# A quantized weight made strip by strip: other steps for the side work of a strip, and later stores in the last one

## The chip, the cores and the metric

The kernel runs on one core of a Trainium2 chip. Its metric is the device time of one execution in microseconds. The core has five engines that run their own instruction lists in order: TensorE (PE in the profile, with its weight loads as PEld), VectorE (DVE), ScalarE (ACT), GpSimd (POOL) and SyncE (SP), which here only issues DMAs. Engines wait for each other by semaphores.

## The reference, cut to what matters

```python
# cond: x (4096 tokens x 2048), weight (2048 x 2048), codebook of 32 values
delta = lora_B @ lora_A * (32 / 64)
wg = (weight + delta).reshape(O, I // 128, 128)
normalized = wg / exp(scale_log)                   # a scale for each group of 128
idx = searchsorted(thresholds, normalized)         # thresholds: middles of the sorted codebook
quantized = codebook[idx]
w = (quantized - normalized) + normalized          # the straight-through form
w_eff = (w * scale).reshape(O, I) + delta
y = x @ w_eff.T
# ffn
result = y @ W_base.T + bias
probs = softmax(y @ router.T)                      # 8 experts
mixed = sum over experts of probs * (y @ A.T @ core)
out = x + result + (mixed @ B.T) * 2
```

All of it is computed in 32 bits. As nothing non-linear lies between y and W_base, the kernel multiplies the two weights first, and the tokens with the product afterwards.

## The kernel before, in words

**First stage.** The 2048 x 2048 quantized weight is made in 16 strips of 128 columns (NS = 16, loop `for i in range(NS)`, line 755). A strip is one tile `w` of 128 partitions x 16 groups x 128, that is 128 x 2048 numbers, with a second tile `a` for the result. Tiles `a` are three, tiles `w` two.

The codebook lookup is a series of 31 selects: for each threshold r, ScalarE writes a mask of 8 bits ("above", line 549: a scaled Relu that is positive where w is over the threshold), and VectorE overwrites `a` with the next codebook value where the mask is set (`copy_predicated`, line 550). There are four mask buffers. Of strip i VectorE does r = 4 to 30, 27 selects of 128 x 2048, in `quantize` (line 554). The levels r = 0 to 3 are done while the strip before is quantized, in halves of 8 groups (f = 0 and 1), by ScalarE and GpSimd: `scalar_level` (lines 512 to 524: Relu, Sign, and a scaled copy, on ScalarE), `pool_levels` (lines 534 and 535) and `last_level` (539). In strips 6 to 15 the level r = 3 of the second half is left to VectorE as a select of half size at the strip's beginning (`half_step`).

**What a strip needs first.** `load_w` (line 391) fetches w by SP's queue; `delta` (404) multiplies the low-rank factors of one half on TensorE into the tile `d`, of which there is one in PSUM, so that the second half has to wait until ScalarE has read the first; `scaled` (498) is that read, into `a`; `normalize` (504) adds it to w and multiplies by the inverse scale on GpSimd (lines 506 and 429).

**What a strip needs after.** `straight_through` (564) does subtract, add and multiply (lines 572 to 574) on GpSimd in two halves, in the last strip on VectorE in four quarters. Then `products` (742) multiplies the strip on TensorE with the four 512-column blocks b of W_base, in pairs (2, 0) and (3, 1), each in four chunks c of four groups (`multiply`, line 614, matmuls at line 621). The first chunk of a pair needs the groups 0 to 3 of `a`. Blocks 0 and 1 of W_base stay in SBUF; 2 and 3 are streamed again for each strip, one piece a chunk, in three buffers (`load_piece`, line 487). A pair ends with `low_rank` (606), the low-rank part of the product, at line 609. `keep` (652) copies a finished block out of PSUM on ScalarE and stores it to DRAM. `multiply_router`, `router_parts`, `router_sum` and `keep_router` do the same for the router's few columns, `route` (671) multiplies them with tokens. There are three PSUM banks for the tiles of the pairs and the router.

**Order by hand.** `at` is a table of steps; `behind(r, f, ...)` puts a call at step r, and `quantize` makes the calls of step r just after it has issued the mask and select of level r + 4. While strip i is quantized, its steps hold: the preparation of strip i + 1, the products of strip i - 1, the end of the products of strip i - 2 (its last chunk stands before step 0), and, from strip 5 on, one column block of finished strips that is taken through sums on GpSimd (`outer_w`, `inner_pair`) and stored by SP (`put`, three DMAs or five a pair). Each engine gets its instructions in this order, and waits in it.

**After the last strip** (lines 843 to 870) come its products, evacuations and stores, `late_columns` for blocks 0 and 2 of the last four strips, and the second stage begins: tokens times the combined weight, 196 products in a twofold scheme of seven (a fast matrix multiplication), bound to TensorE. The sums for blocks 1 and 3 (lines 1190 to 1204) are still done then.

Of the kernel before, what the change touches and what calls it, by code (L numbers as in the profile page):

```python
# [21 lines left out]
P = 128  # L22
# [6 lines left out]
NL = 4  # L29
# [154 lines left out]
def adaln_ffn_kernel(  # L184
# [29 lines left out]
    nc = tc.nc  # L214
    D, N = xT.shape
    NS, _, NM, _ = weight.shape
# [34 lines left out]
    strip = [j * NK + k for k in range(NK) for j in range(4)]  # L251
# [114 lines left out]
    with ExitStack() as sa:  # L366
# [195 lines left out]
            assert not at, at  # L562

        def straight_through(i):
            last = i == NS - 1
            n = 4 if last else 2
            for h in range(n):
                m = ts(h, NM // n)
                w, a = strips[i]["w"][:, m, :], strips[i]["a"][:, m, :]
                sc = scale[:, strip[i], m].unsqueeze(2).to_broadcast([P, NM // n, P])  # L570
                v = nc.vector if last else nc.gpsimd
                v.tensor_tensor(a, a, w, ALU.subtract)  # L572
                v.tensor_tensor(a, a, w, ALU.add)  # L573
                v.tensor_tensor(a, a, sc, ALU.mult)  # L574
# [70 lines left out]
        def router_parts(i):  # L645
            nc.scalar.copy(raw, strips[i]["r"][:, 0:P])

        def router_sum(i):

            nc.tensor.matmul(strips[i]["r"][:, P : P + RP], raw, stack, start=True, stop=True)  # L650

        def keep(i, b):
            out = spool.tile([P, 4, BC], F32, tag="out", name=f"out_{i}_{b}")
            nc.scalar.copy(out.rearrange("p q c -> p (q c)"), strips[i][b])  # L654
            (nc.scalar if i == NS - 1 else nc.sync).dma_start(wc_dram[i // 4][b][:, i % 4], out)

        def keep_router(i):
            nc.scalar.copy(rac[:, strip[i], :], strips[i]["r"][:, P : P + RP])
# [83 lines left out]
        def products(i, bs, c):  # L742

            for b in bs:
                multiply(i, b, c)
            if c == NC - 1:
                low_rank(i, bs)
# [7 lines left out]
        for i in range(NS):  # L755
            at = {}

            def behind(r, f, *args):
                at.setdefault(r, []).append(lambda: f(*args))

            if i > 1:

                products(i - 2, (3, 1), NC - 1)
                route(i - 2, 0)
                behind(0, load_route, i - 2, 1)
                behind(2, keep, i - 2, 3)
                behind(3, keep, i - 2, 1)
            if i + 1 < NS:
                delta(i + 1, 0)
                if i > 0:  # L770
                    behind(1, load_w, i + 1, 2)
                behind(4, scaled, i + 1, 0)
                behind(4, normalize, i + 1, 0)
                behind(10, scaled, i + 1, 1)
                behind(10, normalize, i + 1, 1)
                for r, f, parts in ((0, 0, (11, 12, 13)), (NL - 1, 0, (14, 15, 18)), (0, 1, (19, 20, 21))):
                    for n, p in enumerate(parts):
                        behind(p, scalar_level, i + 1, f, r, n)
                behind(14, pool_levels, i + 1, 0)
                behind(19, last_level, i + 1, 0)  # L780
                behind(21, pool_levels, i + 1, 1)
            if i > 0:


                behind(9, load_route, i - 1, 0)
                if i == NS - 1:
                    behind(9, load_route, i - 1, 1)
                for c in range(2):
                    behind(2 + 3 * c, products, i - 1, (2, 0), c)
                if i + 1 < NS:  # L790
                    behind(7, delta, i + 1, 1)
                if i > 1:
                    behind(8, route, i - 2, 1)
                for c in range(2, NC):
                    behind(2 + 3 * c, products, i - 1, (2, 0), c)
                behind(13, multiply_router, i - 1)
                behind(16, keep, i - 1, 2)
                behind(17, keep, i - 1, 0)
                for c in range(NC - 1):
                    behind((17, 20, 22)[c], products, i - 1, (3, 1), c)  # L800
                behind(19, router_sum, i - 1)
                behind(23, keep_router, i - 1)
                behind(18, router_parts, i - 1)
                if i + 2 < NS:
                    behind(20, load_la, i + 2)
            else:
                behind(3, nc.vector.reciprocal, rflat[:, NM:], flat[:, NM:])
                behind(7, delta, i + 1, 1)
                behind(22, lora_columns, 0)
                behind(24, lora_columns, 1)  # L810
                behind(25, lora_router)
            for n, (g, b) in enumerate(made.get(i, [])):
                step_of = (3, 5, 10, 13, 17, 23, 25) if len(made[i]) == 1 else (
                    (4, 6, 8, 9, 10, 12, 13) if n == 0 else (17, 19, 21, 22, 23, 24, 25)
                )

                def begin(g, b):
                    columns(
                        g, b,
                        ypool.tile([P, 2048], F32, tag="up", name=f"up_{g}_{b}"),  # L820
                        ypool.tile([P, 1536], F32, tag="more", name=f"more_{g}_{b}"),
                    )
                    fetch(g, b)

                def inner_pair(g, b, ms):
                    z = zp.tile([P, 1024], F32, tag="z", name=f"z_{g}_{b}_{ms[0]}")
                    inner_some(nc.gpsimd, g, b, ms, z)

                behind((0, 14)[n], begin, g, b)
                r = step_of  # L830
                behind(r[0], outer_w, nc.gpsimd, g, b)
                behind(r[1], inner_pair, g, b, PAIRS[0])
                behind(r[1], inner_pair, g, b, PAIRS[1])
                behind(r[2], put, g, b, PAIRS[0])
                behind(r[3], put, g, b, PAIRS[1])
                behind(r[4], inner_pair, g, b, PAIRS[2])
                behind(r[4], inner_pair, g, b, PAIRS[3])
                behind(r[5], put, g, b, PAIRS[2])
                behind(r[6], put, g, b, PAIRS[3])
            quantize(i, at)  # L840
            straight_through(i)

# [12 lines left out]
        for bs in ((2, 0), (3, 1)):  # L855
            for c in range(NC):
                products(last, bs, c)
            if bs[0] == 2:
                multiply_router(last)
                router_parts(last)  # L860
            for b in bs:
                keep(last, b)
            if bs[0] == 2:
                router_sum(last)
                keep_router(last)
                late_columns()
        for h in range(2):
            route(last, h)
        for h in range(2):
# [411 lines left out]
```

## Time and profile before

| | us |
|---|---|
| median of three runs | 2672.97 (2670.01 to 2674.29) |
| the profiled execution | 2666.77 |
| its span | 2665.0 |

| engine | busy us (share) |
|---|---|
| TensorE | 2503.9 (94%) |
| VectorE | 1549.0 (58%) |
| GpSimd | 1367.2 (51%) |
| ScalarE | 1130.1 (42%) |

The page's second part cuts the span in 40 slices of 66.6 us with the busy share of each in tenths. Its fifth part has a row for each group of equal instructions: line, engine, operation, output and input, how many; behind the bar the busy time, the mean of one in ns, and the idle time before them with what ended most of it. A view of waits sums them by who waited for whom: total us, how often, the longest. The chain of waits follows the work that ended last back through its releasers: start, us, what. A timeline has start, us, engine, line, operation and how many were merged; in brackets, the idle time before and what ended it.

### The profile page before, as it was taken

What the parts mean: (1) busy time and instruction counts of PE and PEld (TensorE: products, weight loads), DVE (VectorE), ACT (ScalarE), POOL (GpSimd) and SP (SyncE); (2) the same over time, 40 slices, a digit from 0 to 9 for tenths busy, and PEclk for the clock granted to TensorE, in tenths of its full rate; (3) what the DMA queues carried; (4) which work ended last, traced back from release to release, by engine and by line L of the source; (5) the groups of instructions that cost most, each with busy time, mean ns of one, the idle gap of its engine ahead of it and who ended that gap; (6) DMA issues with size and microseconds to landing.
All of it is one profiled execution on the core that took longest, in us unless ns stands there. A gap on an engine that the chain in (4) does not pass through costs nothing.

```text
span 2665.0 us, 26423 instructions
## 1 busy us (share of the span) xinstructions
PE 2503.9 (94%) x10576; PEld 1704.1 (64%) x10576; DVE 1549.0 (58%) x990; ACT 1130.1 (42%) x796; POOL 1367.2 (51%) x783
## 2 busy tenths in 40 slices
PE   5499999999999999999999999999999999999999
PEld 2244444444444444345888888888888888888887
DVE  9999999999999999973433223242133332224221
ACT  7899999999999999930000000000000000000000
POOL 5777778889888888745313140042320323202224
PEclk9799999999999999999999999999999999999999
DMA  8255457776777777699844666536675455854554
GB/s 317 102 177 185 168 181 252 233 241 228 234 243 249 235 231 227 217 327 347 323 174 173 218 245 232 187 142 213 244 234 194 157 206 177 279 208 173 194 199 158
DMA packets 225979, 581.08 MB, mean 218 GB/s; under 512 B 20600, under 2 KB 121728, under 8 KB 182720
## 3 DMA queue, kind: packets, MB, share of 16 engines
q1 hardware_dynamic: 219296, 557.96, 61.1%
q0 software_dynamic: 4960, 14.95, 1.6%
q10 hardware_dynamic: 1600, 6.49, 0.7%
q8 instruction: 83, 1.36, 0.2%
q14 instruction: 40, 0.33, 0.0%
HBM read 477.62 MB, written 101.71 MB: 217 GB/s over the span
## 4 chain that ended last, share of the span: by engine, by line
PE 62%; ACT 17%; DVE 8%; POOL 7%; DMA 3%; issue 2%; SPq 0%; DVEq 0%; ACTq 0%; POOLq 0%
PE z L954 49%; ACT above L549 11%; PE m L621 10%; DVE a L550 7%; ACT sg L516 2%; ACT sg L519 2%; POOL a L572 1%; POOL a L573 1%; PE z L984 1%; ACT a L521 1%; POOL lv L534 1%; POOL a L574 1%; POOL a L535 1%; DMA xA<-in_xT 1%; DMA wc_dram<-out 1%
## 5 line engine op out<-in xcount | busy, mean ns | idle before, releaser
L550 DVE COPY_PREDICATED a<-above,step 128x2048 f32<-128x2048 uint8 (+1 forms) x448 | 1090.2, 2436 | 61.1 <-ACT above L549 19.3
L549 ACT ACTIVATE above<-w,neg_t 128x2048 fp8e5<-128x2048 f32 (+1 forms) x448 | 872.4, 1976 | 55.1 <-DVE a L550 44.5
L954 PE MATMUL z<-t,s 128*128 128x256 f32 x3584 | 791.4, 380 | 2.0 <-DVE u L1036 1.7
L954 PEld LDWEIGHTS z<-t,s 128*128 128x128 f32 x3584 | 677.5, 190 | 105.5 <-issue 13.2
L621 PE MATMUL m<-wbp,a 128*128 128x512 f32 x1024 | 502.1, 636 | 115.0 <-POOL a L574 101.0
L621 PE MATMUL m<-wb,a 128*128 128x512 f32 x1024 | 462.1, 594 | 4.4 <-ACT out L654 4.4
L621 PEld LDWEIGHTS m<-wbp,a 128*128 128x128 f32 x1024 | 202.6, 204 | 370.9 <-issue 239.7
L621 PEld LDWEIGHTS m<-wb,a 128*128 128x128 f32 x1024 | 194.5, 191 | 247.1 <-issue 242.4
L1034 ACT COPY m<-z 128x1024 f32<-128x1024 f32 x28 | 28.4, 1013 | 759.2 <-PE z L954 759.2
L1045 POOL TENSOR_TENSOR c<-u,m 128x1024 f32<-128x1024 f32 x16 | 50.1, 3130 | 443.8 <-DVE u L1042 422.4
L954 PE MATMUL z<-xA,s 128*128 128x256 f32 x1152 | 254.6, 379 | 0.0
L534 POOL TENSOR_SCALAR lv<-w,past,rise 128x1024 f32<-128x1024 f32 x65 | 245.9, 3783 | 3.7
L954 PEld LDWEIGHTS z<-xA,s 128*128 128x128 f32 x1152 | 218.8, 190 | 30.5 <-issue 0.8
L1045 POOL TENSOR_TENSOR M<-u,m 128x1024 f32<-128x1024 f32 x8 | 24.5, 3068 | 328.9 <-DVE u L1042 288.2
L954 PE MATMUL z<-xC,s 128*128 128x256 f32 x768 | 169.7, 379 | 0.0
L954 PE MATMUL z<-xB,s 128*128 128x256 f32 x768 | 169.7, 379 | 0.0
L535 POOL TENSOR_TENSOR a<-a,lv 128x1024 f32<-128x1024 f32 x65 | 154.3, 2374 | 27.1 <-ACT a L521 21.0
L1036 DVE TENSOR_TENSOR u<-z,m 128x1024 f32<-128x1024 f32 x28 | 34.3, 1224 | 218.5 <-issue 175.0
L1040 ACT COPY m<-z 128x1024 f32<-128x1024 f32 x28 | 28.3, 1011 | 308.8 <-PE z L954 308.8
L954 PEld LDWEIGHTS z<-xC,s 128*128 128x128 f32 x768 | 145.9, 190 | 19.8
L954 PEld LDWEIGHTS z<-xB,s 128*128 128x128 f32 x768 | 145.9, 190 | 19.8
L1042 DVE TENSOR_TENSOR u<-z,u 128x1024 f32<-128x1024 f32 x28 | 34.3, 1223 | 119.8 <-PE z L954 81.3
(213 smaller groups left out, 1958.0 us busy)
## 6 DMA issues: line engine op xcount, KB each, us to landing
s<-s_dram SPq DMA_DIRECT2D x196, 1024.0 KB, 4.9
wbp<-in_wbT SPq DMA_DIRECT2D x131, 1024.0 KB, 5.4
xs<-in_xT SPq DMA_DIRECT2D x64, 512.0 KB, 6.5
xA<-in_xT SPq DMA_DIRECT2D x24, 1024.0 KB, 9.4
s_dram<-z SPq DMA_DIRECT2D x84, 256.0 KB, 6.2
xB<-in_xT SPq DMA_DIRECT2D x16, 1024.0 KB, 10.4
outT<-M SPq DMA_DIRECT2D x16, 1024.0 KB, 12.5
w<-in_weight SPq DMA_DIRECT2D x30, 512.0 KB, 5.2
```

Of the source, the lines that this page charges most:

```text
L516: nc.scalar.activation(strips[i]["sg"], q, AF.Relu, bias=neg_t[:, r : r + 1], scale=GAIN)
L519: nc.scalar.activation(sg, sg, AF.Sign)
L534: v.tensor_scalar(lv, half(i, f, "w"), past[:, r : r + 1], rise[:, r : r + 1], ALU.is_gt, ALU.mult)
L535: v.tensor_tensor(a, a, lv, ALU.add)
L549: nc.scalar.activation(above[:, c], q, AF.Relu, bias=neg_t[:, r : r + 1], scale=GAIN, saturate=False)
L550: nc.vector.copy_predicated(a, above[:, c].bitcast(U8), step[:, r : r + 1].to_broadcast([P, F // n]))
L621: nc.tensor.matmul(ps, strips[i]["a"][:, CM * c + m, :], t[:, m, :], start=c == 0 and m == 0, stop=False)
L954: nc.tensor.matmul(z[:, c, :], s[:, k, ts(c, P)], rhs[:, k, :], start=not more and k == 0 and c % PER == 0, stop=k == NK - 1 and c % PER = ...
L1034: nc.scalar.copy(temp("m1", o), z["a"])
L1036: nc.vector.tensor_tensor(temp("u2", o), z["b"], state["m1", o], ALU.add)
L1042: nc.vector.tensor_tensor(temp("u3", o), z["d"], state["u2", o], ALU.add)
L1045: lambda d: nc.gpsimd.tensor_tensor(d, state["u3", o], state["m5", o], ALU.add),
```

## The change

Four things change, all in the first stage.

1. `straight_through`: GpSimd does the first half in two parts of four groups, the second half whole.
2. Steps. The second half's `delta` goes from step 7 to step 3, `scaled` to 3 and 5 (before 4 and 10), both halves of `normalize` to 6 (before 4 and 10). The level r = 0 of the first half goes to 9, 10, 11, that of the second half to 13, 16, 17, the level 3 of the first half to 20, 21, 23, and GpSimd's levels to 11 and 17, with `last_level` at 23. The chunks of the pair (2, 0) go to 4, 6, 8, 11 (before 2, 5, 8, 11), and that pair's evacuations to 14 and 15 (before 16 and 17).
3. A column's `outer_w` goes from step 3 to 5, its pairs to 8, 14 and twice 24 (before 5, 5, 17, 17), its puts to 10, 16, 25, 26 (before 10, 13, 23, 25). In strip 15, which has two columns, the steps keep their values.
4. `keep` is split into `evacuate` and `store`. In the last strip both blocks of a pair are evacuated first. The stores of the first pair, the router's sum and `late_columns` come behind the first chunk of the second pair.

```diff
         def straight_through(i):
             last = i == NS - 1
-            n = 4 if last else 2
-            for h in range(n):
-                m = ts(h, NM // n)
+            v = nc.vector if last else nc.gpsimd
+            for m in (0, 4), (4, 8), *(((8, 12), (12, 16)) if last else ((8, 16),)):
+                n = m[1] - m[0]
+                m = slice(*m)
                 w, a = strips[i]["w"][:, m, :], strips[i]["a"][:, m, :]
-                sc = scale[:, strip[i], m].unsqueeze(2).to_broadcast([P, NM // n, P])
-                v = nc.vector if last else nc.gpsimd
+                sc = scale[:, strip[i], m].unsqueeze(2).to_broadcast([P, n, P])
...
-        def keep(i, b):
+        def evacuate(i, b):
             out = spool.tile([P, 4, BC], F32, tag="out", name=f"out_{i}_{b}")
             nc.scalar.copy(out.rearrange("p q c -> p (q c)"), strips[i][b])
-            (nc.scalar if i == NS - 1 else nc.sync).dma_start(wc_dram[i // 4][b][:, i % 4], out)
+            strips[i]["out", b] = out
+
+        def store(i, b, q=nc.sync):
+            q.dma_start(wc_dram[i // 4][b][:, i % 4], strips[i]["out", b])
+
+        def keep(i, b):
+            evacuate(i, b)
+            store(i, b)
...
                 behind(2, keep, i - 2, 3)
-                behind(3, keep, i - 2, 1)
+                behind(4, keep, i - 2, 1)
             if i + 1 < NS:
                 delta(i + 1, 0)
                 if i > 0:
                     behind(1, load_w, i + 1, 2)
-                behind(4, scaled, i + 1, 0)
-                behind(4, normalize, i + 1, 0)
-                behind(10, scaled, i + 1, 1)
-                behind(10, normalize, i + 1, 1)
-                for r, f, parts in ((0, 0, (11, 12, 13)), (NL - 1, 0, (14, 15, 18)), (0, 1, (19, 20, 21))):
+                behind(3, scaled, i + 1, 0)
+                behind(3, delta, i + 1, 1)
+                behind(5, scaled, i + 1, 1)
+                for f in range(2):
+                    behind(6, normalize, i + 1, f)
+                for r, f, parts in ((0, 0, (9, 10, 11)), (0, 1, (13, 16, 17)), (NL - 1, 0, (20, 21, 23))):
                     for n, p in enumerate(parts):
                         behind(p, scalar_level, i + 1, f, r, n)
-                behind(14, pool_levels, i + 1, 0)
-                behind(19, last_level, i + 1, 0)
-                behind(21, pool_levels, i + 1, 1)
+                behind(11, pool_levels, i + 1, 0)
+                behind(17, pool_levels, i + 1, 1)
+                behind(23, last_level, i + 1, 0)
...
                 for c in range(2):
-                    behind(2 + 3 * c, products, i - 1, (2, 0), c)
-                if i + 1 < NS:
-                    behind(7, delta, i + 1, 1)
+                    behind((4, 6, 8, 11)[c], products, i - 1, (2, 0), c)
...
-                behind(16, keep, i - 1, 2)
-                behind(17, keep, i - 1, 0)
+                behind(14, keep, i - 1, 2)
+                behind(15, keep, i - 1, 0)
                 for c in range(NC - 1):
                     behind((17, 20, 22)[c], products, i - 1, (3, 1), c)
-                behind(19, router_sum, i - 1)
-                behind(23, keep_router, i - 1)
+                behind(20, router_sum, i - 1)
+                behind(24, keep_router, i - 1)
...
-                step_of = (3, 5, 10, 13, 17, 23, 25) if len(made[i]) == 1 else (
-                    (4, 6, 8, 9, 10, 12, 13) if n == 0 else (17, 19, 21, 22, 23, 24, 25)
+                step_of = ((5, 8, 10), (12, 14, 16), (24, 24, 25), (24, 25, 26)) if len(made[i]) == 1 else (
+                    ((4, 6, 8), (6, 6, 9), (10, 10, 12), (10, 10, 13)) if n == 0 else
+                    ((17, 19, 21), (19, 19, 22), (23, 23, 24), (23, 23, 25))
                 )
...
         for bs in ((2, 0), (3, 1)):
             for c in range(NC):
                 products(last, bs, c)
+                if bs[0] == 3 and c == 0:
+                    router_sum(last)
+                    keep_router(last)
+                    for b in (2, 0):
+                        store(last, b, nc.scalar)
+                    late_columns()
             if bs[0] == 2:
                 multiply_router(last)
+            for b in bs:
+                evacuate(last, b)
+            if bs[0] == 2:
                 router_parts(last)
-            for b in bs:
-                keep(last, b)
-            if bs[0] == 2:
-                router_sum(last)
-                keep_router(last)
-                late_columns()
+        for b in (3, 1):
+            store(last, b, nc.scalar)
```

More of the change, by code (lines that the diff above doesn't have):

```diff
@@ L794, in adaln_ffn_kernel @@
                 for c in range(2, NC):
-                    behind(2 + 3 * c, products, i - 1, (2, 0), c)
+                    behind((4, 6, 8, 11)[c], products, i - 1, (2, 0), c)
                 behind(13, multiply_router, i - 1)
-                behind(16, keep, i - 1, 2)
-                behind(17, keep, i - 1, 0)
+                behind(14, keep, i - 1, 2)
+                behind(15, keep, i - 1, 0)
                 for c in range(NC - 1):
                     behind((17, 20, 22)[c], products, i - 1, (3, 1), c)
-                behind(19, router_sum, i - 1)
-                behind(23, keep_router, i - 1)
+                behind(20, router_sum, i - 1)
+                behind(24, keep_router, i - 1)
                 behind(18, router_parts, i - 1)
@@ L807, in adaln_ffn_kernel @@
                 behind(3, nc.vector.reciprocal, rflat[:, NM:], flat[:, NM:])
-                behind(7, delta, i + 1, 1)
                 behind(22, lora_columns, 0)
@@ L830, in adaln_ffn_kernel @@
                 r = step_of
[L831 to L839, printed above, removed]
+                behind(r[0][0], outer_w, nc.gpsimd, g, b)
+                for k, pair in enumerate(PAIRS):
+                    behind(r[k][1] if k else r[0][1], inner_pair, g, b, pair)
+                    behind(r[k][2], put, g, b, pair)
             quantize(i, at)
```

## The prediction

> **What bounds the kernel now.** I read the page first, for which engine is full in which part of the span.
>
> ```profile
> PE   5499999999999999999999999999999999999999
> ...
> DVE  9999999999999999973433223242133332224221
> ...
> L550 DVE COPY_PREDICATED a<-above,step 128x2048 f32<-128x2048 uint8 (+1 forms) x448 | 1090.2, 2436 | 61.1 <-ACT above L549 19.3
> L549 ACT ACTIVATE above<-w,neg_t 128x2048 fp8e5<-128x2048 f32 (+1 forms) x448 | 872.4, 1976 | 55.1 <-DVE a L550 44.5
> ```
>
> VectorE is full up to slice 17 (17.6 x 66.6 = 1173 us): the 16 quantized strips, in series. After that TensorE is full. TensorE's 9s in the first stretch are no bound: its work of a strip ends about when VectorE's next strip begins, and it waits for it. So the time is VectorE's strips, a handover, and some 1375 us of TensorE that the change doesn't touch.
>
> How long a strip is, I read from the chain of waits: GpSimd's first subtraction (L572) starts 0.1 us after VectorE's last select.
>
> ```profile
> 815.22 2.40 POOL a L572
> ...
> 886.90 2.39 POOL a L572
> ```
>
> 71.7 us, and so for the strips around it. The least a strip can take: 27 selects of 2.473 us with the 0.10 us between dependent ones (starts lie 2.575 apart), 69.5 us, and from strip 6 on a half select, 1.42: 70.9. So VectorE loses only 0.7 us a strip. The waits of the stretch 0 to 1185 us say the same:
>
> ```profile
> ACT a L502 <- PE d L410: 49.8, 14, 5.5
> ...
> DVE a L550 <- ACT above L549: 19.3, 49, 0.6
> ```
>
> All that better timing of ScalarE can win is 19.3 us less the ordinary 0.1 of 49 gaps, 14 us. ScalarE stands 49.8 us waiting for the low-rank half, and VectorE hardly notices: four mask buffers let ScalarE be ahead. What has to be found is whether the new order keeps that lead.
>
> **One strip, laid out.** t runs from VectorE's start of strip 11 at 815.0. The timeline, engine by engine:
>
> ```profile
> 817.55 2.00 ACT L549 ACTIVATE above<-w,neg_t 128x2048 fp8e5<-128x2048 f32 x1
> 819.46 0.57 ACT L654 COPY out<-m 128x512 f32<-128x512 f32 x1
> ...
> 839.92 1.02 ACT L502 ACTIVATE a<-d 128x1024 f32<-128x1024 f32 x1 [3.12 <-PE d L410]
> ...
> 842.73 1.14 ACT L516 ACTIVATE sg<-w,neg_t 128x1024 bf16<-128x1024 f32 x1
> ```
>
> ```profile
> 822.09 6.16 PE L621 MATMUL m<-wbp,a 128*128 128x512 f32 x8 [4.75 <-POOL a L574]
> ...
> 854.73 1.13 PE L609 MATMUL m<-lora_c,la 64*128 64x512 f32 x4
> ```
>
> Reader's points: TensorE starts the products at t = 7.1, its first eight passes take 6.16 instead of 3.43 (the next eight start at 828.31, those after at 831.75), and the pair (2, 0) is done at t = 40.9. ScalarE copies it out only at 857.30 (t = 42.3), as step 16 comes: 1.4 us of slack. A mask on ScalarE costs 1.89 from start to start (next start 0.11 before its end); an evacuation 0.47, a scaled half 0.91, the passes of a level 1.04, 0.95 and 1.13.
>
> **The change, part by part.**
>
> (a) *GpSimd's first half in quarters.* Six instructions for three: 128x512 takes 1.28 (L320 row), the product half of 1.90: 1.28+1.28+0.95 and two gaps of 0.08, 3.7 us a quarter, 7.3 against 6.75 a half. The first quarter is ready at t = 3.9 instead of 7.0; everything behind on GpSimd comes 0.5 later. It also frees w 0.5 later, for SP's weight load that holds SP to t = 11.8 in both versions; the pieces behind it are three ahead of their use, which covers it.
>
> (b) *delta of the second half at step 3.* It now stands on TensorE ahead of the products, and has to wait until ScalarE has scaled the first half out of the one PSUM tile (step 3). Queued behind it: every product of the strip. ScalarE's mask of step 3 starts at 817.55 and is followed at 819.46 (t = 4.46): there the scaled half runs now, to 5.5. Delta takes 1.16. So products start at 6.7, not 3.9: part (a)'s gain is spent by (b). ScalarE's 3.1 us wait at step 10 is gone, and 1.16 us leaves the middle of the products.
>
> (c) *TensorE's slow start.* The pair (3, 1) before it begins at 857.93 (t = 42.9) now; after the change at 39.0 + 1.5 for the router, as the copies at 14 and 15 have freed its banks. 40.5 + 27.7 + 1.13 + route 1.06 + the first delta 1.16 is 71.6, that is t = -1.4 of a next strip 73 us on, and TensorE stands nearly 7 us before the second delta. After 4.4 to 5.6 us of standing the trace always shows half speed (6.16 instead of 3.43 here; 8.99 instead of 6.87 for 16 passes at 249.87): a loss of 2.1 to 2.7, I take 2.4. After 3.45 (at 180.23) it shows none. The Trainium skill, "TensorE: Matmul & The Clock Gate", Part 1, has half the clock after an idle window of 3.4 us until 3.4 us of work: by that rule the loss is 1.7. The row decides, the rule is the mild end.
>
> (d) *Pair (2, 0) is done* at 5.55 + 1.16 + 2.4 + 8 x 3.43 + 0.22 (identity) + 1.06 (route) + 1.13 = 39.0: 1.9 earlier than now.
>
> (e) *Its evacuation moves from step 16 to 14.* ScalarE is in order, so the mask of r = 19 waits behind it: 39.0 + 0.47 + 2.0 + 0.1 = 41.6. VectorE wants that mask, the 16th full one, at 1.42 + 15 x 2.575 = 40.0. It is 1.6 late, and VectorE waits. The other way round: the copy has 1.4 us of slack now, the pair comes 1.9 sooner, and two steps take 5.15: -1.9. The two reckonings agree to 0.3.
>
> (f) *No lead covers it.* Both normalizations now follow outer_w (GpSimd, step 6): 0.1 + 7.3 + 6.7 + 5.0 + 4.3 puts the first at t = 23.4, where it was 23.2, but the level pass that reads it moves from step 11 to 9. ScalarE gets there after the mask of r = 13, whose buffer is free at 1.42 + 6 x 2.575 = 16.9: at 18.8. It waits 4.6 us, and its lead is gone at r = 14 (ready 26.7, wanted 27.2).
>
> (g) *Levels at 13, 16, 17 and 20, 21, 23.* From r = 19 to r = 22 ScalarE needs 1.89 x 3 + 0.47 + 0.95 + 1.13 = 8.2, VectorE 7.7: another 0.5 late. Behind step 18 there is little, and ScalarE regains its lead before the strip ends.
>
> A strip with half step: 70.9 + 1.6 + 0.5 = 73.0 against a mean of 71.6 (457.08 to 1101.59 over strips 6 to 14): +1.4, nine times, **+12.6**. Strips 2 to 5 have no half step: scaled half one half mask earlier (pair done at 38.0), mask due at 38.6, ready at 40.5: 69.5 + 1.9 + 0.5 = 71.9, four times 287.6 against 283.7 (173.37 to 457.08): **+3.9**. Strip 1 has no earlier strip's copies on ScalarE, so its pair is done 2 us sooner: about 70.0 against 72.6, **-2.6**. Strip 15 prepares nothing: 0. Together **+13.9**.
>
> (h) *GpSimd's and SP's other moves.* Pairs and puts of a finished column go from steps 17 to 25 to 24 to 26, behind last_level at 23. GpSimd has 7 us left in a strip (it waits 5.9 at L572), and SP has nothing urgent before the weight load at t = 11.8. Nothing, unless the last pair ends later than 12 us into the next strip. The products' pieces and wc_dram stores move with their steps, behind the same weight load: nothing.
>
> (i) *Handover.*
>
> ```profile
> 1214.72 0.34 ACTq L655 DMA_DIRECT2D wc_dram<-out  x1
> 1215.10 0.59 ACT L654 COPY out<-m 128x512 f32<-128x512 f32 x1 [7.77 <-DMA xA<-in_xT]
> ...
> 1215.74 0.80 PE L621 MATMUL m<-wb,a 128*128 128x512 f32 x1 [4.43 <-ACT out L654]
> ```
>
> A store on ScalarE's queue holds the second copy, and TensorE waits 4.43 for its bank. Copies first, stores later: TensorE wins 4.43 and 0.35 (L650's wait), and loses some 1.4 to a slow start on the last strip (its wait there grows from 1.76 to about 5). But the stores now follow four chunks of products: 1208 + 6.9 + 0.7 puts the second at 1216.2, 0.5 later, and from there the chain runs over late columns and VectorE to TensorE's wait at 1288.53. Bounds -3.4 and +0.5; I take **-1**, nearer the chain.
>
> Sum: +13.9 - 1 = +13 on the profiled execution's 2666.8 (span 2665.0 and 1.8 around it): 2680. That execution lies 6.2 under the median shown, so on the median, 2673 + 13 = **2686 us**. What this kernel's measurement tells from no change is about 0.2%, 5 us.
>
> **Rivals.**
> *TensorE doesn't start slowly (faster).* Place: delta at t = 5.55. Then the pair is done at 36.6, before ScalarE comes for it (23.5 + 1.04 + 5 x 1.89 + 0.95 + 1.13 + 1.04 = 37.1), the mask is in time, strips take 71.3 and 69.5. It decides from a pair done before 37.4, 1.6 less than I have. (71.3 - 71.6) x 9 - 5.7 - 2.6 - 3 for the handover: -14, 2659. For it: the 3.45 us gap that cost nothing. Against: thirteen gaps over 4.4 us that all cost 2 us or more, and this one is longer. 11 in 100.
> *Loss and gain meet (same).* With the rule's 1.7 in (c) each of 13 strips costs 0.7 less, which leaves 13.9 - 9.1 = +5, and the handover gives its -3.4: 2674. 12 in 100.
> *The forecast (slower).* 2679 to 2695 by the ends in (c) and (i) and 0.3 us in a strip's layout; 77 in 100, of which 5 are for GpSimd or the late stores binding as well: ScalarE's wait in (f) grows by each us that the weight load lands late, 14 strips, over 2697.
>
> So faster 0.11, same 0.12, slower 0.77. The range that leaves out no more than 2 in 10: 2668 to 2697.
>
> **What would show it.** L572 starts 73 us apart in strips 7 to 14 (right) or at most 71.7 (wrong). VectorE's waits for masks grow from 19.3 to about 33. ScalarE's copy (L655 after) waits for TensorE's L610 in nearly every strip, and its level pass L516 for GpSimd's L429. TensorE's L410 waits 6 to 7 us for ScalarE's L502, the products no longer for GpSimd, and the first eight passes still exceed 5 us. No 4.43 us wait near the handover. The forecast is wrong if the pair (2, 0) is done by t = 37.4, or if ScalarE meets the strip's start without its lead.

## The result, and the profile after

| | median, us | range |
|---|---|---|
| before | 2672.0 (20 executions) | 2668.5 to 2676.8 |
| after | 2678.4 (20 executions) | 2673.9 to 2682.8 |

The ratio is 1.0024, 95% interval 1.0018 to 1.0030: slower by 6.3 us, between 4.8 and 8.0. The forecast was 13 us slower. Direction and mechanism held; the size is under half of what was said. The profiled execution of after took 2677.88 us (span 2676.0), 0.5 under its median; that of before lies 5 us under its own, so the pair of profiles shows 11 us where the medians show 6. The first profile of the kernel with late copies (below) fell on an execution of 2718 us at a lower granted clock (0.935 over the span, where others have 0.977 to 0.979), so its strips are read from a second one.

The page of the profile after, lines that answer to those shown of before:

```profile
PE   5599999999888889998999999999999999999999
...
DVE  9999999999999999972533222242123322214221
...
L550 DVE COPY_PREDICATED a<-above,step 128x2048 f32<-128x2048 uint8 (+1 forms) x448 | 1089.9, 2436 | 68.8 <-ACT above L549 25.7
L549 ACT ACTIVATE above<-w,neg_t 128x2048 fp8e5<-128x2048 f32 (+1 forms) x448 | 867.3, 1972 | 30.4 <-DVE a L550 20.6
```

The selects take what they took; VectorE stands 68.8 us ahead of them instead of 61.1, and its waits for masks are 25.7 where they were 19.3 (the forecast: about 33). TensorE, which is not the bound here, shows 8s where it showed 9s.

GpSimd's first subtraction, which starts as VectorE ends a strip (timeline; start, duration):

```profile
528.59 1.28 POOL L573 TENSOR_TENSOR a<-a,w 128x512 f32<-128x512 f32 x1 [3.44 <-DVE a L550]
...
600.47 1.28 POOL L573 TENSOR_TENSOR a<-a,w 128x512 f32<-128x512 f32 x1 [3.42 <-DVE a L550]
...
672.64 1.28 POOL L573 TENSOR_TENSOR a<-a,w 128x512 f32<-128x512 f32 x1 [3.80 <-DVE a L550]
...
746.10 1.28 POOL L573 TENSOR_TENSOR a<-a,w 128x512 f32<-128x512 f32 x1 [3.43 <-DVE a L550]
```

Strips 7, 8 and 9 are 71.9, 72.2 and 73.5 us long. Strips 6 to 14 have a mean of 72.50; before it was 71.61, forecast was 73.0. Adding up VectorE's end of strip to end of strip:

| strips | before, us | after, us | measured | forecast |
|---|---|---|---|---|
| 1 | 72.6 | 69.7 | -2.9 | -2.6 |
| 2 to 5 | 283.7 | 286.1 | +2.4 | +3.9 |
| 6 to 14 | 644.5 | 652.5 | +8.0 | +12.6 |
| 15 | 71.0 | 71.0 | 0 | 0 |
| together | | | +7.4 | +13.9 |

The last strip ends at 1172.5 us before and at 1179.9 after. Other profiles below with the same strips put the first at 1173.6 (handover alone) and the second at 1181.7 (strips alone) and 1182.3 (stores on SP): the +7.4 of this pair could as well be 6 to 10.

The waits of the same stretch as before, 0 to 1185 us (total, times, longest):

```profile
PE d L410 <- ACT a L502: 126.8, 15, 28.8
...
ACT sg L516 <- POOL w L429: 67.3, 14, 6.4
ACT out L655 <- PE m L610: 27.6, 16, 4.6
...
DVE a L550 <- ACT above L549: 25.7, 39, 2.1
...
PE m L622 <- POOL a L575: 6.2, 1, 6.2
```

TensorE's second delta waits for ScalarE's scaled half (b), 5.8 to 7.0 us in a strip. ScalarE's level pass waits 67.3/14 = 4.8 us for GpSimd's normalization (f). The copy waits for the pair's low-rank product in every strip (e). The products wait for GpSimd only once, in strip 15 (6.2). All the rest is the forecast's.

Now two neighbouring strips, 8 (t = 0 at 600.3) and 9 (t = 0 at 672.5). TensorE, ScalarE's copy and VectorE (timeline):

```profile
605.77 2.08 PE L410 MATMUL d<-la,lora_BT_sb 64*128 64x128 f32 x16 [6.64 <-ACT a L502]
607.78 4.25 PE L622 MATMUL m<-wbp,a 128*128 128x512 f32 x8
...
677.93 2.08 PE L410 MATMUL d<-la,lora_BT_sb 64*128 64x128 f32 x16 [7.02 <-ACT a L502]
679.95 5.70 PE L622 MATMUL m<-wbp,a 128*128 128x512 f32 x8
```

```profile
638.34 0.59 ACT L655 COPY out<-m 128x512 f32<-128x512 f32 x1 [0.51 <-PE m L610]
...
712.19 0.59 ACT L655 COPY out<-m 128x512 f32<-128x512 f32 x1 [2.18 <-PE m L610]
```

```profile
633.04 7.63 DVE L550 COPY_PREDICATED a<-above,step 128x2048 f32<-128x2048 uint8 x3 [0.46 <-ACT above L549]
640.86 7.69 DVE L550 COPY_PREDICATED a<-above,step 128x2048 f32<-128x2048 uint8 x3 [0.19 <-ACT above L549]
649.10 20.55 DVE L550 COPY_PREDICATED a<-above,step 128x2048 f32<-128x2048 uint8 x8 [0.55 <-ACT above L549]
...
714.70 7.67 DVE L550 COPY_PREDICATED a<-above,step 128x2048 f32<-128x2048 uint8 x3 [1.87 <-ACT above L549]
```

In both strips delta starts at t = 5.48, as forecast (5.55), and runs at half speed (2.08 for 1.16). In strip 8 the pair (2, 0) is done at t = 38.0, in strip 9 at 39.7; the copy goes off within 0.05 of it, and VectorE waits 0.19 and 1.87 us for the mask of r = 19 behind the copy (the rows of strip 8 at 633.04 and 649.10 are its waits at r = 16 and 22). One strip lies under the forecast's 39.0 and 1.6, the other over it. What differs is how long TensorE ran at half clock. Stretches of 3.41 us with TensorE's busy time in them and the granted clock (window, us, PE, PEld, DVE, ACT, POOL, clock, DMA share, GB/s):

```profile
602.09:605.50 3.41, 0.00 (x0) 0.00 (x0) 3.31 (x2) 3.41 (x4) 3.29 (x3) 0.50 0.95 339
605.50:608.91 3.41, 3.14 (x18) 2.40 (x19) 3.31 (x2) 3.41 (x4) 3.30 (x3) 0.50 1.03 366
608.91:612.33 3.42, 3.42 (x10) 1.50 (x9) 3.21 (x3) 3.42 (x3) 3.34 (x2) 1.00 0.34 115
...
677.18:680.59 3.41, 2.65 (x17) 2.29 (x18) 3.31 (x2) 3.41 (x4) 3.25 (x4) 0.50 0.91 305
680.59:684.01 3.42, 3.42 (x5) 1.35 (x4) 3.32 (x2) 3.42 (x3) 3.34 (x2) 0.50 0.45 157
684.01:687.42 3.41, 3.41 (x10) 1.55 (x9) 3.20 (x3) 3.41 (x3) 3.33 (x3) 1.00 0.41 86
```

The clock changes on a grid of 3.41 us. In strip 8 work came 0.27 us into a window and the clock was full from the next; in strip 9 it came 0.75 us into one, and the clock stayed at half for another window. Seven of strips 6 to 14 are like strip 8, two (9 and 12) like strip 9.

Handover, TensorE (timeline) and ScalarE's stores:

```profile
1182.14 5.37 PE L622 MATMUL m<-wbp,a 128*128 128x512 f32 x8 [4.47 <-issue]
...
1214.66 3.70 PE L622 MATMUL m<-wbp,a 128*128 128x512 f32 x8
...
1259.86 16.23 PE L961 MATMUL z<-t,s 128*128 128x256 f32 x64 [7.00 <-issue]
...
1299.49 7.17 PE L961 MATMUL z<-t,s 128*128 128x256 f32 x32 [2.69 <-DVE u L1043]
```

```profile
1222.25 7.00 ACTq L659 DMA_DIRECT2D wc_dram<-out  x2
```

The 4.43 us wait for the copy is gone, as forecast. New is that TensorE stands 7.0 us later and starts slowly again (16.23 where 64 such passes took 13.98 before). The second store was issued 6.7 us after the first; the chain of waits has a fetch of late columns ahead of it that lands at that moment:

```profile
1212.36 16.49 DMA late<-wc_dram
1228.92 4.83 DMA wc_dram<-out
```

That fetch took 16.5 us. So the late columns reach VectorE 57.8 us after its last strip, 53.7 before.

### The profile page after: what moved, and what is told of

Same layout as the page of the kernel before. It is cut to its first block, busy times and chain, and to the rows that moved or that the text cites. A ratio compares the mean times of both kernels' runs of the same rounds, so it can differ in the third digit from the quotient of the medians.

```text
span 2676.0 us, 26447 instructions
## 1 busy us (share of the span) xinstructions
PE 2503.0 (94%) x10576; PEld 1711.4 (64%) x10576; DVE 1548.4 (58%) x990; ACT 1125.4 (42%) x796; POOL 1374.7 (51%) x828
## 4 chain that ended last, share of the span: by engine, by line
PE 70%; ACT 18%; DVE 6%; DMA 3%; issue 2%; POOL 1%; SPq 1%; DVEq 0%; POOLq 0%; ACTq 0%
PE z L961 49%; PE m L622 17%; ACT above L549 14%; DVE a L550 5%; PE z L991 1%; PE d L410 1%; ACT sg L519 1%; DMA late<-wc_dram 1%; PE m L610 1%; ACT a L521 1%; DMA s_dram<-late_z 1%; ACT out L655 1%; PE acc L682 1%; ACT a L502 0%; ACT sg L516 0%
## 5 line engine op out<-in xcount | busy, mean ns | idle before, releaser
L550 DVE COPY_PREDICATED a<-above,step 128x2048 f32<-128x2048 uint8 (+1 forms) x448 | 1089.9, 2436 | 68.8 <-ACT above L549 25.7
L622 PE MATMUL m<-wbp,a 128*128 128x512 f32 x1024 | 487.2, 620 | 11.3 <-POOL a L575 6.2
L622 PEld LDWEIGHTS m<-wbp,a 128*128 128x128 f32 x1024 | 197.2, 199 | 255.3 <-issue 242.9
L410 PE MATMUL d<-la,lora_BT_sb 64*128 64x128 f32 x512 | 54.4, 371 | 139.9 <-ACT a L502 126.8
## 6 DMA issues: line engine op xcount, KB each, us to landing
outT<-M SPq DMA_DIRECT2D x16, 1024.0 KB, 12.4
```

Source lines behind the costliest of these rows:

```text
L410: nc.tensor.matmul(d[:, 4 * h + n, :], lora_BT_sb[rows, f, n, :], strips[i]["la"][rows], start=True, stop=True,)
L550: nc.vector.copy_predicated(a, above[:, c].bitcast(U8), step[:, r : r + 1].to_broadcast([P, F // n]))
L622: nc.tensor.matmul(ps, strips[i]["a"][:, CM * c + m, :], t[:, m, :], start=c == 0 and m == 0, stop=False)
```

## Experiments

Two questions were open: how the 6.3 us divide between strips and handover, and which of the steps (c) to (g) makes the strips long. Times below are against the kernel before in the same series (2671 to 2672 us); strips are read from the timelines, as above.

### The handover alone

```diff
 before, with evacuate and store split, and the last strip's order as in the change
+                if bs[0] == 3 and c == 0:
+                    router_sum(last)
+                    keep_router(last)
+                    for b in (2, 0):
+                        store(last, b, nc.scalar)
+                    late_columns()
```

> The kernel before with the changed handover alone (part 4: copies together, router's copy and stores behind the first products of the second pair); strips as before. Theory A (the second store of the first pair is issued only after a fetch that lands late, because the two share a completion semaphore): 3 to 5 us over the kernel before, and in the trace the two stores start about 6 us apart. Rival B (the forecast's step (i): the handover gains by the 4.43 us wait that goes, and all of the +6.3 us is the strips'): 1 to 3 us under the kernel before.

Measured: ratio 1.0005 (0.9997 to 1.0013), +1.3 us with -0.8 to +3.5. That lies between the two expectations, and no change can be told from none; Rival B's gain of 1 to 3 us is outside the interval, Theory A's 3 us just inside. The stores go out together here:

```profile
1216.30 0.82 ACTq L658 DMA_DIRECT2D wc_dram<-out  x2
```

The order is that of after, so the order alone doesn't make the second store late. Here the fetch of late columns that was issued 9.9 us ahead of the first store landed after 10.0 us; in after it took 16.5 and in the run with TensorE kept busy 14.1, and there the second store was issued within 0.1 us of its landing. In this profile the first products with u begin 115.1 us after VectorE's last strip (1288.69 less 1173.63), 116.0 before: the forecast's -1, within what two executions differ by.

### The strips alone

```diff
 after, with the last strip's order as before
```

> The changed kernel with the handover as it was (parts 1 to 3 alone). Theory A: what is left of the +6.3 us when the handover's 3 to 5 us are taken off, 2 to 4 us over the kernel before; strips 6 to 14 keep their length of 72.5 us in the trace. Rival B: all of it, +6 to +9 us. The forecast's own figure for the strips was +13.9 us.

Measured: 1.0028 (1.0016 to 1.0039), +7.4 us, strips 6 to 14 at 72.53. Rival B's size: the strips carry all of it. From VectorE's last strip to the first products with u it is 119.5 us, as long as in the profile of after (119.6), though the store isn't late:

```profile
1225.69 6.62 PE L622 MATMUL m<-wb,a 128*128 128x512 f32 x8 [4.43 <-ACT out L655]
...
1301.12 9.05 PE L957 MATMUL z<-t,s 128*128 128x256 f32 x28 [3.65 <-DVE u L1039]
```

The 4.43 us are back, and the end is no later. In these two profiles, what TensorE saves at one wait of the handover it stands at the next.

### The copies of the pair (2, 0) back at their old steps

```diff
-                behind(14, keep, i - 1, 2)
-                behind(15, keep, i - 1, 0)
+                behind(16, keep, i - 1, 2)
+                behind(17, keep, i - 1, 0)
```

> The changed kernel with only the copies of the pair (2,0) back at steps 16 and 17, behind ScalarE's masks of these steps. Theory A (the copy at step 14 stands on ScalarE until the pair is done at t = 38 to 39 and the masks behind it come late, which is what a strip loses): strips fall to 70 to 71 us, 12 to 20 us under the changed kernel, so faster than the kernel before by 6 to 14 us. Rival B (the lead is lost to GpSimd's level at step 9 and to the later normalizations, steps (f) and (g), and the copy only uses time that is lost anyway): within 4 us of the changed kernel.

> The changed kernel with the copies of the pair (2, 0) at steps 16 and 17, a second profile. Theory A (the strips of 71.4 us in the profile taken first are this kernel's own): strips 6 to 14 at 71.0 to 71.5, strips 2 to 4 at 69.4 to 69.7, VectorE's strips end at 1163 to 1166 us, and its waits for masks under 10 us. Rival B (that profile was lengthened): strips 6 to 14 at 70.7 to 71.0.

Measured: 0.9961 (0.9947 to 0.9974), 2660.7 us: 10.1 faster than before and 16 to 18 faster than after, which is Theory A. The second profile's execution took 2659.3 us, with strips 2 to 5 at 69.9, 6 to 14 at 71.38, the strips' end at 1163.2 (after: 1179.9), and

```profile
ACT sg L516 <- POOL w L429: 60.2, 14, 5.0
...
ACT out L655 <- PE m L610: 21.3, 13, 5.5
...
DVE a L550 <- ACT above L549: 6.3, 13, 1.2
```

Two lines of the change, (e), cost more than the whole change loses: without them the same change makes the kernel faster. The wait for GpSimd, (f), is still there (60.2), but without the copy ahead of the mask VectorE feels little of it. One thing more moves with the copies: the banks come free later, the pair (3, 1) starts later, and TensorE stands only 1.4 us ahead of the second delta, so the slow start is gone from the strip's beginning and the pair (2, 0) is done at 37.6 in the mean. This run alone doesn't tell which of the two saves the time; the run with all three moves, below, does.

### TensorE kept busy while it waits

```diff
-            if c == 0:
+            if c == 0 and b not in strips[i]:
...
+        def keep_busy(i):
+            strips[i][2] = psum_m.tile([P, OQ], F32, tag="m", name=f"m_{i}_2")
+            for _ in range(8):
+                nc.tensor.matmul(strips[i][2], ident, wb[0][:, 0, :], start=True, stop=True)
...
+                if i > 1:
+                    behind(0, keep_busy, i - 1)
                 behind(3, delta, i + 1, 1)
```

> The changed kernel with eight more matmuls of 512 columns on TensorE at step 0 (their results are overwritten), which fill the 6.7 us in which it waits for ScalarE. They add no work to any other engine. Theory A (the wait lets TensorE's clock fall, and the half-clock stretch behind it is what makes the pair (2,0) end at t = 38 to 39): no half-clock stretch at the strip's beginning, the pair ends near t = 36.6, masks wait no more for the copy at step 14, strips 70 to 71.5 us, 8 to 18 us under the changed kernel. Rival B (the clock falls for another reason than the wait, or the pair's end is not what the strip waits for): within 3 us of the changed kernel, or slower, if the added matmuls hold back delta of the second half.

The kernel computes all that it did; the added products are overwritten. Measured: 0.9975 (0.9965 to 0.9985), 2664.3 us: 13 to 14 faster than after, 6.5 faster than before. Strip 8 (timeline):

```profile
594.34 7.13 PE L753 MATMUL m<-wb,ident 128*128 128x512 f32 x16
601.79 1.16 PE L410 MATMUL d<-la,lora_BT_sb 64*128 64x128 f32 x16 [0.32 <-ACT a L502]
602.88 3.70 PE L622 MATMUL m<-wbp,a 128*128 128x512 f32 x8
```

More work, and the time falls: delta takes 1.16 for 2.08, the first eight passes 3.70. The pair is done at t = 36.6 to 36.8 in all of strips 6 to 14, the copy goes when ScalarE comes for it, at 37.5, and the strips take 71.41. This is the forecast's first rival made by hand, which had 36.6, 37.1 and 71.3. Theory A stands. With the slow start gone, the early copy does no harm.

### Delta of the second half back at step 7

```diff
-                behind(3, delta, i + 1, 1)
-                behind(5, scaled, i + 1, 1)
-                for f in range(2):
-                    behind(6, normalize, i + 1, f)
+                behind(10, scaled, i + 1, 1)
+                behind(6, normalize, i + 1, 0)
+                behind(10, normalize, i + 1, 1)
...
+                    behind(7, delta, i + 1, 1)
```

> The changed kernel with delta of the second half back at step 7, in the middle of the products, and its scaling and normalization back at step 10. Copies, levels and handover as changed. Theory A (delta at step 3 makes TensorE stand 6.7 us, and this brings the slow start): TensorE's standing time at the strip's beginning falls under 4.5 us, fewer or no half-clock stretches, pair (2, 0) done at 37.5 to 38.5, strips near 71.9, which is 4 to 8 us under the changed kernel. Rival B (the pair is late because of the work ahead of its products, wherever delta stands): strips at 72.5 and within 2 us of the changed kernel.

Measured: 1.0019 (1.0010 to 1.0028), +6.0 us; strips 6 to 14 at 72.25. Theory A's gain did not come; the time is Rival B's. TensorE still stood 5.4 to 6.2 us (now for GpSimd's first quarter, to t = 4.0), the half-clock windows stayed, and the pair was done at 37.5 in the mean, 1.2 sooner than after. But the copy went no sooner than 38.3: the scaled half at step 10 now comes in ScalarE's order ahead of the copy, behind the wait for GpSimd. The pair is the last to come at step 14 in some versions, ScalarE itself in others; the masks behind are about as late either way.

### The first half's normalization ahead of the outer products

```diff
-                for f in range(2):
-                    behind(6, normalize, i + 1, f)
+                behind(4, normalize, i + 1, 0)
+                behind(6, normalize, i + 1, 1)
```

> The changed kernel with only the first half's normalization moved from step 6 to step 4, ahead of GpSimd's outer products; copies at steps 14 and 15 and handover as changed. Theory A (while the copy at step 14 stands until the pair is done, it is the last wait before the late mask, and ScalarE's wait for GpSimd at step 9 lies in its shadow): ScalarE's wait for GpSimd shrinks by 2 us in the later strips, VectorE's waits for masks stay at 23 to 27 us, time within 3 us of the changed kernel. Rival B (the wait at step 9 is a loss of its own, as the gain of the run with all three moves suggests): 5 to 8 us under the changed kernel.

Measured: 1.0024 (1.0013 to 1.0036), +6.3 us, the same as the change.

```profile
ACT out L655 <- PE m L610: 51.1, 15, 5.3
ACT sg L516 <- POOL w L429: 46.2, 14, 4.6
DVE a L550 <- ACT above L549: 27.0, 37, 2.2
```

ScalarE waits 21 us less for GpSimd (1.5 a strip) and 23.5 us more for TensorE. Theory A: step (f) lies in the shadow of step (e).

### All three moves: late copies, early normalization, stores on SP

```diff
 after, with the two edits above (copies at 16 and 17, normalization at 4), and
-                    for b in (2, 0):
-                        store(last, b, nc.scalar)
-                    late_columns()
...
             if bs[0] == 2:
+                for b in bs:
+                    store(last, b, nc.sync)
+                late_columns()
```

> The changed kernel with three moves: copies of the pair (2, 0) at steps 16 and 17, the first half's normalization at step 4, ahead of GpSimd's outer products (step 6 before), and the first pair's stores on SP. With the copies alone the strips measured 71.4 us. Theory A (what is left of a strip over VectorE's own 69.5 to 70.9 us is ScalarE's level at step 9 waiting for GpSimd's late normalization, step (f)): strips 6 to 14 at 70.7 to 71.0, another 3 to 8 us off the strips' end, and with the handover 18 to 26 us under the changed kernel, 2652 to 2660 us. Rival B (GpSimd's outer products now come too late instead, or the lead is not what the strips lose by): no faster than with the copies alone, 2660 to 2664 us.

Measured: 2653.6 us, 0.9939 (0.9925 to 0.9953): 17.4 us faster than before (12.6 to 20.0), 24 to 25 faster than after: Theory A. Strips 2 to 5 take 69.5, strips 6 to 14 71.1 (0.1 over what was expected), the strips end at 1159.5, and the page has

```profile
L550 DVE COPY_PREDICATED a<-above,step 128x2048 f32<-128x2048 uint8 (+1 forms) x448 | 1091.3, 2440 | 47.1 <-DVE a L550 2.3
L549 ACT ACTIVATE above<-w,neg_t 128x2048 fp8e5<-128x2048 f32 (+1 forms) x448 | 867.5, 1972 | 50.0 <-DVE a L550 40.2
```

VectorE's first releaser is itself, and ScalarE waits for VectorE's buffers (40.2), as an engine does that is ahead. VectorE's waits for masks in the strips are 0.9 us in all. The early normalization, worth nothing while the copies stood at step 14, is worth 3.7 us at the strips' end (1163.2 to 1159.5) with them late; in the profile with the late copies alone VectorE still waits 0.4 us at r = 16 in most of strips 6 to 14, here it doesn't. TensorE starts slowly here too in strips 8 to 14 (in 9 and 10 the pair is done at 39.2 and 39.6), but the copy comes at 39.6 to 40.3 and rarely has to wait (7.4 us in all strips). Strips 9 and 10 take 70.9 us each: in the run before this one, with the early copy, a pair done at 39.7 or 39.8 made strips of 73.5 to 73.8. A late pair costs nothing when its copy is late too, so it is the copy's place, and not only TensorE's start, that saves the time.

### The stores on SP alone

The kernel after, with the last of the three edits above.

> The changed kernel, with the first pair's two stores of the last strip issued on SP right behind the two copies, and the late columns' fetches behind them, instead of on ScalarE behind the first products of (3, 1). Strips as in the changed kernel. Theory A (the second store is issued 7 us after the first because it waits on a completion semaphore that it shares with a fetch in flight, so the late columns reach VectorE 4 us later and TensorE stands 7.0 us and then starts slowly, 2.25): 4 to 9 us under the changed kernel, no 7 us wait of TensorE at the first products with t. Rival B (the end of the handover is set by the string of small transfers behind the late columns, which take 50 to 65 us with much scatter): within 3 us of the changed kernel.

Measured: 1.0020 (1.0013 to 1.0026), +5.9 us, 0.4 under the change's +6.3: Rival B.

```profile
1257.79 14.05 PE L961 MATMUL z<-t,s 128*128 128x256 f32 x64 [3.26 <-issue]
...
1296.45 8.86 PE L961 MATMUL z<-t,s 128*128 128x256 f32 x32 [3.89 <-DVE u L1043]
```

The 7.0 us become 3.3, the next wait grows from 2.7 to 3.9 and now starts slowly itself (8.86 for 7.17). From VectorE's last strip to the first products with u it is 114.1 us in this profile, 5.5 less than after, of which the slow start takes 1.7; the medians show next to none of the rest.

### GpSimd's first half whole

```diff
-            for m in (0, 4), (4, 8), *(((8, 12), (12, 16)) if last else ((8, 16),)):
+            for m in ((0, 4), (4, 8), (8, 12), (12, 16)) if last else ((0, 8), (8, 16)):
```

> The changed kernel with GpSimd's first half in one part of eight, as before (part (a) undone). Theory A (forecast's step (a): what the quarters give is spent by delta at step 3, which holds the products longer): within 2 us of the changed kernel, the strips 1 to 14 unchanged. Rival B (the quarters carry the products' start where delta does not hold it, in strips 1 and 15): 3 to 5 us slower.

Measured: 1.0080 (1.0066 to 1.0094), +22 us, 15 to 16 over the change: both expectations missed. Strips 6 to 14 hardly move (72.68), but 2 to 5 take 73.3 instead of 71.5, strip 1 2.6 more and strip 15 2.1 more. In strips 1 to 5 there is no half select, delta comes early, and the products then wait for GpSimd after all, to t = 7.0; with the quarters they start at 5.1 to 6.4, and in strip 15 at 4.0; the clock's half windows are three, not two, in strips 2 to 5. Strip 3:

```profile
249.96 2.08 PE L410 MATMUL d<-la,lora_BT_sb 64*128 64x128 f32 x16 [5.79 <-ACT a L502]
252.58 6.66 PE L622 MATMUL m<-wbp,a 128*128 128x512 f32 x8 [0.55 <-POOL a L575]
```

A wait of 0.55 us makes this strip 2.1 longer (73.95 for 71.85): it falls into the second half-clock window, and a third follows (t = 2.8 to 13.0, where after has 2.6 to 9.4).

### The kernel before with early copies

```diff
 before, with
-                behind(16, keep, i - 1, 2)
-                behind(17, keep, i - 1, 0)
+                behind(14, keep, i - 1, 2)
+                behind(15, keep, i - 1, 0)
```

> The kernel before with only the copies of the pair (2, 0) moved from steps 16 and 17 to steps 14 and 15. Theory A (step (e)'s reckoning: the mask behind the copy is ready at the pair's end + 0.47 + 2.0 + 0.1 and wanted at 40.0; the pair ends at t = 40.9 there): the mask 3.5 late, of which ScalarE's and TensorE's next strip give nothing back, so 3 to 3.5 us in each of strips 2 to 14 and 40 to 48 us over the kernel before. Rival B (ScalarE has more lead in the kernel before and takes the wait from it): under 15 us.

Measured: 1.0184 (1.0169 to 1.0200), +48.7 us; strips 6 to 14 at 75.05 for 71.61, the pair done at 40.8. Theory A, just over its 40 to 48.

```profile
ACT out L654 <- PE m L609: 57.9, 16, 8.1
...
DVE a L550 <- ACT above L549: 70.8, 49, 4.3
```

Step (e) alone, in the kernel where the pair is later, costs nearly eight times what the whole change does. The copy's time and the strip's length go together in all versions with it at step 14 (means of strips 6 to 14; four of them here, the others lie on the same line):

| version | pair done, t | copy starts, t | strip, us |
|---|---|---|---|
| TensorE kept busy | 36.7 | 37.5 | 71.4 |
| delta at step 7 | 37.5 | 38.3 | 72.25 |
| after | 38.7 | 38.7 | 72.5 |
| before, early copies | 40.8 | 40.8 | 75.0 |

A strip is some 34 us longer than the time of its first copy.

## Why the prediction was right or wrong

**(a) GpSimd in quarters: half right.** The forecast said its gain is spent by (b). So it is in strips 6 to 14, where delta's half speed and not GpSimd sets the first product (7.49). In strips 1 to 5 and 15 it is not: without the quarters these take 12 us longer, of 13.5 us in all at the strips' end. The sum held it already in the pair's times, so this misled only my expectation of the experiment.

**(b) Delta blocks TensorE: right.** Delta at t = 5.48 (forecast 5.55), standing 6.6 to 7.0 us (forecast nearly 7).

**(c) The slow start: right in kind, and near in its mean by luck.** Forecast 2.4 us of loss in each strip. Without any loss the pair would be done at 5.48 + 1.16 + 27.44 + 0.22 + 1.06 + 1.13 = 36.5, and the run with TensorE kept busy has 36.6 to 36.8. The pair of after lost 1.5 to 2.3 against 36.5 in seven strips of 6 to 14 and 3.2 and 3.3 in two: 1.9 in the seven, 2.2 in all nine. (The first eight passes, which were to stay over 5 us, take 4.25 to 4.9 in the seven and 5.7 and 5.8 in the two, as delta bears 0.92 of it.) The row I took from before was misread by a little: 6.16 is a duration, whose counterpart at full clock is 3.70 and not the distance of starts 3.43, so its loss is 2.5; and by the half clock that was left when work came back, the thirteen gaps of before cost 1.9 to 2.7, not all 2 or more. The row also measured another phase: there the half-clock windows began at t = 5.2 to 5.5, just ahead of the products at 7.05, and ended at 12.0 to 12.4, so 5 us of work went at half clock. After the change TensorE stands from t = -1.4, the windows begin at 1.3 to 3.1, and most end at 8.6 to 9.9, 3.1 to 4.4 us after delta's start. The loss is half of that. The Trainium skill, "TensorE: Matmul & The Clock Gate", Part 1, by whose rule I had 1.7, was nearer for the seven strips; for strips 9 and 12 it is half of what was lost. The page also says that the window runs free of the program, and the granted clock's grid agrees. My mild end, 1.7 for all strips, gave +5 for the strips; they measured +7.4.

**(d), (e) and (g), the length of a strip: the term that failed.** The size that was wrong is (e)'s 1.6 us of VectorE's wait for the mask of r = 19. Over the ordinary 0.1 between selects, it waits 0.7 in the mean of strips 6 to 14 (0.1 to 1.9). For r = 16 it waits 0.33: there (f), which was given no time of its own, holds VectorE up, so that it wants the mask of r = 19 later. (With the early normalization that wait is gone, and at the same pair's end, 38.3 to 38.4, the wait for r = 19 is 0.33 longer.) Together that is 1.0 instead of 1.6; for r = 22, (g), it waits 0.46 (forecast 0.5). Two errors explain the size. The pair, forecast at 39.0, is done at 38.7 in the mean. And 39.0 was to make a strip of 73.0; the strips with the pair at 38.8 (72.6) and 39.7 (73.5) put 39.0 at 72.8. So of the 0.5 us that a strip of 6 to 14 was forecast too long, 0.3 is the pair and 0.2 the layout behind it. Over nine strips that is 4.6 us; strips 2 to 5 (forecast 71.9, measured 71.5) and strip 1 add 1.5 and 0.3. That is the 6.5 between +13.9 and +7.4. The mechanism of (e) is shown from three sides: undone in after, added to before, and disarmed by a pair that is in time.

**(f) Lead gone:** the wait is there (4.8, forecast 4.6), and it is shown to hide behind (e): 1.5 us less of it in a strip bring nothing with the early copy, and 3.7 us over the strips without it.

**(h) Nothing:** no run tests it alone, and none speaks against it.

**(i) Handover -1: not refuted, and not shown.** The strips' +7.4 and the medians' +6.3 leave -1, the handover alone measures +1.3 (-0.8 to +3.5). The forecast didn't see the second store held 6.7 us, nor TensorE's 7.0 us wait; in the profile of after they take back what the 4.43 us gave. Its sum for the second store is wrong as well: 1208 + 6.9 + 0.7 is 1215.6 and not 1216.2, which moves that bound by 0.6 us and decides nothing. From the strips' end to the end of the span, twelve profiles lie between 1491.7 and 1498.6 us, without order between the old handover's code and the new (the two with the stores on SP are among the three shortest): the 3.6 us by which the profile after is longer there is no more than that spread. Which of its small transfers makes an execution long or short stays open.

**The rivals.** The first rival (no slow start) fell for this kernel, and its numbers came true when TensorE was kept busy. The second, strips +5 and handover -3.4, had the better size of the slow start and too large a handover. What the forecast left unsaid is that it stood on the difference of two large terms: every strip's loss is what is left of a pair 2 us sooner against a copy 5 us sooner, and thirteen strips multiply its error.

## What to carry to other kernels

A copy that frees a bank for a late producer should stand, on an in-order engine, behind the work that others wait for: two steps of difference were worth 16 to 18 us here, more than all else in the change. Undo a change part by part even when it loses as a whole, since the good parts (quarters, 15 us) may be hidden by the bad one (early copies), and two waits in a row hide each other: the second pays only once the first is gone. When a loss repeats in every round, look whether it sits at the same phase of something that runs free; a change of the round's length shifts it.

## What the hardware showed that I had not expected

The granted clock changes on a grid of 3.41 us that doesn't heed the program: in strips 2 to 14, stretches at half clock last 3.41, 6.83 or 10.24 us, that is one, two or three windows. Before, a strip of 71.6 us in the mean is nearly 21 of these windows (71.68), so each strip met the grid at nearly the same point (windows from t = 5.2 to 5.5 in strips 7 to 14) and lost the same. At 72.2 us the phase wanders, and some strips pay three half-clock windows for two. In all profiles in which delta ends TensorE's stand in strips 6 to 14, work that came up to 0.29 us into a window ended the half clock with it; work that came 0.31 us into it or later did not. And eight matmuls in each strip, whose result nobody reads, made the kernel 13 to 14 us faster.
